# A convolution-and-attention kernel: SyncE's instructions in source order, queries prepared a slot sooner, and VectorE adding channel chunks ahead of the mean products of the first image

## The chip, the cores and the metric

The kernel runs on one core of one Trainium2 chip. A core has five engines with instruction queues of their own: TensorE (PE) multiplies matrices into PSUM, VectorE (DVE) and ScalarE (ACT) work elementwise on PSUM and SBUF, GpSimd (POOL) and SyncE (SP) here mostly issue DMAs. Each queue is worked off in order; an instruction that waits holds everything behind it. The metric is the device time of one execution in microseconds (us), as the median of several runs.

## The reference

For each of 4 images of 384 channels and 48 x 48 pixels (2304 tokens), in float32:

```python
x_flat = x.reshape(B, C, N).transpose(0, 2, 1)
local = conv_general_dilated(x, conv_w, (1, 1), 'SAME', feature_group_count=C)   # depthwise, 7 x 7
local = local * inv + (bn_beta - bn_mean * inv)                                  # batch norm
qkv = layernorm(x_flat) @ qkv_w.T + qkv_b                                        # 8 heads of 48
q = q + layernorm(local)
out = softmax(q @ k.T * 48 ** -0.5) @ v
result = x_flat + out @ proj_w.T + proj_b
```

So each query is the sum of a projection of the normalised pixel and of the normalised local convolution; the softmax runs over all 2304 tokens of the image.

## The kernel before

**Tiles and stages.** Channels lie on the 128 partitions in three chunks (`CC = 3`). An image's queries are worked in 5 tiles of 8, 10, 10, 10 and 10 pixel rows (384 or 480 tokens); `t` counts the tiles of all images, 0 to 19. Ahead of an image's tiles stands its key phase: six groups of 384 tokens (`g`, or `gk` for images 1 to 3), each making values, keys and raw queries with PE (L556, in `project`) and, for images 1 to 3, the output projection of the image before.

**Slots.** A tile has 12 slots: 4 pairs of heads times 3 parts of 6 key blocks. In a slot PE first makes six blocks of scores (`score`, L940), ScalarE takes their exponentials (L948), and PE then weighs the values with them (`weigh`, L955). The sums go to SBUF by ScalarE (L837, L847), and VectorE adds those of parts 1 and 2 (`sums_add`, L856). All of PSUM is one ring of four buffers of two banks.

**Queries.** The scores multiply at reduced width, so each query is split in a high part, a ScalarE copy (`high_queries`, L808), and a low part, a VectorE subtraction (`low_queries`, L813). SyncE then copies rows within the tile (two DMAs of L818, four of L820) so that both parts stand on the right partitions. `high_queries(t, pair + 1)` stood ahead of the scores of the second slot of a pair, `low_queries(t, pair + 1)` between its weighing and the second half of its convolution work. Pair 0 of the next tile is prepared near the end of the tile: in image 0 by the branch `early`, later by the branch `following`. At slot 0 `gather_tails` copies the fourth pair's rows (8 DMAs, L562). Keys get the same split in the key phase (L646 by ScalarE, L649 by VectorE), and `keys_out` sends the parts by SyncE (L579 to L582) and GpSimd.

**Convolution.** VectorE makes the 49 taps of three chunks, 147 instructions a tile (L306, L302), as one stream. A planner written in the kernel deals them out: every half slot and every fifth of a key group has a `room` in microseconds, every tile a due point, and the rate is the largest need over room. `FIRST_ROOM` is the room of the first point, `("start",)`, between the key phase of image 0 and slot 0. During the key phase of image 0 the taps are counted out by hand (`convolve_first(n)`). The first 10 taps of chunk 0 of tile 0 are made by PE.

**Norm of the convolution.** In image 0 (`early`, tiles 1 to 4, prepared during tiles 0 to 3) the mean over channels is a product with a matrix of 1/384, three chunks accumulated (`mean_kept`, then a ScalarE copy L467): one such mean of the convolution in slot `first` (8 in tile 0, 7 in tiles 1 to 3), one of the squares in the slot after. `root` takes the reciprocal root on ScalarE (L485 to L487), `newton` refines it on VectorE (L493, L494), `local_end` and `query_end` (L785, L794) make the queries. Later images (`following`, `coming`) sum across channels by VectorE and two DMAs of SyncE instead: `out` (L508 writes `parts`, L509 reads it back as `four`, and waits for it), then `few_in` (L518).

**The divisor.** `sums_add` sends the softmax sums to DRAM (L861); `divide` of a later point (slot 2 of the next tile, or key group 1 of the next image) reads them (`rd`, L876), takes the reciprocal on VectorE (L877), writes it (L882) and reads it back as a broadcast (`rb`, L887, L890), by which the tile's output is multiplied (L1246, L1134).

**What sets the order.** `tc.manual_schedule(engines=...)` names the engines whose instructions are kept in the order of the source. These were PE, VectorE and ScalarE; for the loads at the start also SyncE and GpSimd. Everything else on SyncE and GpSimd is put in an order by the framework's planner, which simulates the program. It may set a DMA that is ready early ahead of others that stand before it in the source.

Of the kernel before, what the change touches and what calls it, by code (L numbers as in the profile page):

```python
# [29 lines left out]
OUT_SLOT = 7  # L30
WARM = 14
PE_TAPS = 10
FIRST_ROOM = 14.0

# [11 lines left out]
def unshifted_pass(  # L48
# [16 lines left out]
    nc = tc.nc  # L65
# [7 lines left out]
    NP = NH // 2  # L73
# [20 lines left out]
    work = ctx.enter_context(tc.tile_pool(name="work", bufs=2))  # L94
    dram = ctx.enter_context(tc.tile_pool(name="dram", bufs=2, space=bass.MemoryType.DRAM))
    ps = ctx.enter_context(tc.tile_pool(name="ps", bufs=4, space=bass.MemoryType.PSUM))
    engines = {mybir.EngineType.PE, mybir.EngineType.DVE, mybir.EngineType.Activation}
    ctx.enter_context(tc.manual_schedule(engines=engines))

    def two_banks(name="r"):  # L100
        return ps.tile([P, 2, 512], F32, tag="r", name=name)
# [21 lines left out]
    def load_slab(b, g, parts=1, queue=nc.gpsimd):  # L123
# [7 lines left out]


    loads = ExitStack()
    loads.enter_context(
        tc.manual_schedule(engines={mybir.EngineType.SP, mybir.EngineType.Pool})
    )
    nc.scalar.preload_act_table_set("natural_log_exp_and_others")


# [15 lines left out]
    mean_w = const.tile([P, P], F32, tag="mean_w", name="mean_w")  # L155
# [110 lines left out]
    accs = {}  # L266
# [140 lines left out]
    def convolve(*point):  # L407
        for _ in range(share[point]):
            next(stream)
# [6 lines left out]
    class Norm:  # L416
# [41 lines left out]
        def mean_by_chunk(self, src, m=None):  # L458
            self.m = two_banks()[:, 0, : self.n] if m is None else m
            project(self.m, lambda c: mean_w, lambda c: src[:, c, :])  # L460

        def mean_kept(self, src):

            m = two_banks()[:, 0, : self.n]
            project(m, lambda c: mean_w, lambda c: src[:, c, :])
            self.m = self.buf[:, 0, :]
            nc.scalar.copy(self.m, m)  # L467

        def mean_of(self, src, at):

# [333 lines left out]
    def high_queries(t, p):  # L804
        qs = work.tile([P, 3, GM], HALF, tag="qs", name=f"qs{t}_{p}", bufs=5)
        qs = qs[:, :, : columns_of(t)]
        stacked[t, p] = qs
        nc.scalar.copy(qs[:, 0, :], query_of(t, p))  # L808
# [40 lines left out]
    def sums_add():  # L849

        if not parts_of:
            return
        t, p, i, part = parts_of.popleft()
        ao, ao3, den = outputs[t]
        dst = (ao[:, p, :] if p < CC else ao3)[0 : 64 + HA]
        nc.vector.tensor_add(dst, dst, part[0 : 64 + HA])  # L856
        if i < KB // BATCH - 1:
            return
        for j in range(2):
            r = 64 * j  # L860
            nc.sync.dma_start(out=den[2 * p + j : 2 * p + j + 1], in_=dst[r + HD : r + HA])  # L861
        if p == NP - 1:
            for c in range(CC):
                for r in (0, 64):
                    nc.sync.dma_start(
                        out=ao[r + HD : r + 64, c, :], in_=ao3[r + 16 * c : r + 16 * c + 16]
                    )
# [95 lines left out]
    def score_batch(t, s):  # L963
        p, k0 = s // (KB // BATCH), s % (KB // BATCH) * BATCH
        for kb in range(k0, k0 + BATCH):
            score(t, p, kb)
# [17 lines left out]
    def convolve_first(n):  # L984
        nonlocal n_first
        n_first += n
        for _ in range(n):
            next(stream)
# [62 lines left out]
    for g in range(1, NG):  # L1051

        last = g == NG - 1
        making = from_x(0, g)
        both(making)
        assert not last or n_first >= each - PE_TAPS
        norm = Norm(accs[0] if last else xn[0, g + 1])
        norm.mean_by_chunk(norm.src)
        if last:
            added = output_bias()  # L1060
        if g in (3, 5):
            keep_stack(0, g // 2 - 1)
        convolve_first(8)
        norm.centre()
        norm.squares()
        both(making)
        if not last:
            convolve_first(7)
            both(making)
        norm.mean_by_chunk(norm.buf)  # L1070
        norm.root()
        if last:
            convolve_first(9)
        lows_out(1)
        if last:
            both(making)
        both(making)
        convolve_first(4 if last else 10)
        if not last:
            lows_out(2)  # L1080
        if last:
            local_end(0, norm.newton())
        else:
            norm.scale(norm.newton())
        next(making)
        if last:
            query_end(0)
            high_queries(0, 0)
            low_queries(0, 0)
        next(making)  # L1090
        if not last:
            convolve_first(7)
# [5 lines left out]
    for t in range(NT):  # L1098
# [72 lines left out]
        first, second = norm_slots(t)  # L1171
        for s in range(NSLOT):
            pair, part = divmod(s, KB // BATCH)
            if part == 1 and pair < NP - 1:
                high_queries(t, pair + 1)
            if early and s == first + 3:
                high_queries(t + 1, 0)
            score_batch(t, s)
            if s == 0:
                gather_tails(*reversed(queries[t]))  # L1180
            if s == 0 and g == 0:
                keep_stack(b, 2)
            if (s or g) and (s < NSLOT - 2 or g < NA - 1):
                load_keys(b, s + 2)
            if s == 2 and g:
                rb = divide(t - 1)
            if s == 0 and coming:
                load_x(b + 1, g - begins(b + 1))
            if s == NSLOT - 4 and g == NA - 1:
                if next_image:  # L1190
                    ao = fetch(b, 0)
                    for gx in range(NG - later(b + 1), NG - 1):
                        load_x(b + 1, gx)
                else:
                    places = [("acc", 3)] * 3 + [("sq", 2)] * 2 + [("qs", 5)]
                    aos = []
                    for i in range(NG):
                        load_residual(b, i, *places[i])
                        aos.append(fetch(b, i) if i < NG - 1 else outputs[t][0])
            if coming and s == X_SLOTS[1] + 1:  # L1200
                norm_x.scale(norm_x.few_newton())
            if following and s == second + 1:
                local_end(t + 1, norm.few_newton())
                query_end(t + 1)
                high_queries(t + 1, 0)
            if coming and s == X_SLOTS[0] + 1:
                jobs.extend(norm_x.square_jobs())
            if following and s == first + 1:
                jobs.extend(norm.square_jobs())
            if coming and s == X_SLOTS[1]:  # L1210
                norm_x.few_variance()
            if following and s == second:
                norm.few_variance()
            if early and s == first + 3:
                low_queries(t + 1, 0)
            convolve("slot", t, s, 0)
            sums_add()
            if early and s == first + 1:
                norm.centre()
                jobs.extend(norm.square_jobs())  # L1220
            if early and s == first + 2:
                local_end(t + 1, norm.newton())
                query_end(t + 1)
            if coming and s == X_SLOTS[1]:
                norm_x.few_root()
            if following and s == second:
                norm.few_root()
            weigh_batch(t, s)
            if early and s == first:
                norm = Norm(accs[t + 1])  # L1230
                norm.mean_kept(norm.src)
            if early and s == first + 1:
                norm.mean_kept(norm.buf)
                norm.root()
            if part == 1 and pair < NP - 1:
                low_queries(t, pair + 1)
            convolve("slot", t, s, 1)
            if following and s == second + 1:
                low_queries(t + 1, 0)
            if coming and s == X_SLOTS[0]:  # L1240
                norm_x.few_centre()
            if following and s == first:
                norm.few_centre()
            if s == OUT_SLOT and g:
                ao = outputs[t - 1][0]
                nc.vector.tensor_mul(ao, ao, rb)  # L1246
                hold(t - 1)
            if coming and s == X_SLOTS[0] - 2:
                norm_x = Norm(xn[b + 1, g - begins(b + 1)])
                norm_x.sum()  # L1250
                norm_x.out()
            if coming and s == X_SLOTS[0] + 1:
                norm_x.sum_squares()
                norm_x.out()
            if following and s == first - 2:
                norm = Norm(accs[t + 1])
                norm.sum()
                norm.out()
            if following and s == first + 1:
                norm.sum_squares()  # L1260
                norm.out()
# [559 lines left out]
```

## Time and profile before

| | us |
|---|---|
| runs (3) | 2777.67, 2779.15, 2781.53; median 2779.15 |
| the profiled execution | 2776.61 |
| its span | 2774.7 |
| TensorE / VectorE / ScalarE busy in it | 2738.0 / 2348.4 / 1633.0 |
| mean granted TensorE clock | 0.996 |

The kernel is timed by the runs; the profile shows one execution. In it a line such as `L306 DVE ...` gathers all instructions of one source line, engine, operation and shape, with the engine's busy time and the mean duration of one. A wait is told as "who waited, <- for whom: total us, times, longest". "DVE ... <- ACT ..." is an engine that waited for another; "<- DMA" for a transfer's landing. SyncE's own instructions appear as `SPq`: they wait and issue, and do not count as busy. In this profile image 0's key phase ends at about 165 us and its tiles at 729 us. A slot of PE lasts 9.07 us in a tile of 480 tokens and 7.38 us in one of 384, and in images 1 to 3 every slot but the first of an image has this length.

### The profile page before, as it was taken

Reading aid. Unit: us, or ns where it says so; the run is one execution under the profiler, and the core shown is the slowest. Engines: PE = TensorE matmul, PEld = TensorE weight load, DVE = VectorE, ACT = ScalarE, POOL = GpSimd, SP = SyncE. Lnnn points to the kernel's source line nnn. Section 1 sums busy time; section 2 is a strip of 40 time slices with the busy share of each in tenths; the row PEclk is TensorE's granted clock in tenths of the full one; section 3 lists DMA queues with packets and bytes.
Section 4 is the critical chain, followed back from the end, with each engine's and each line's share of the span. In section 5 each row is a group of like instructions: output and inputs, shape, how many; then the busy total and the mean of one; then the engine's idle time right before and its main releaser. Section 6 shows DMA issues by size and latency. Waiting matters only on the chain.

```text
span 2774.7 us, 46317 instructions
## 1 busy us (share of the span) xinstructions
PE 2738.0 (99%) x16402; PEld 1552.4 (56%) x16402; DVE 2348.4 (85%) x4100; ACT 1633.0 (59%) x2262; POOL 695.5 (25%) x1273
## 2 busy tenths in 40 slices
PE   9989999999999999999999999999999999999999
PEld 6555555555555655555556555555555565555555
DVE  7998988989999999989888899898899889987212
ACT  4346666666424676776732567677652276676662
POOL 5641101111375111110257311101117711110110
PEclk9999999999999999999999999999999999999999
DMA  7345534445455454454545554545535545444442
GB/s 142 94 117 133 138 108 126 127 121 143 129 151 151 127 149 132 128 136 133 158 125 145 150 141 122 138 126 145 138 117 166 136 133 132 141 127 133 142 147 73
DMA packets 163297, 369.14 MB, mean 133 GB/s; under 512 B 61488, under 2 KB 112208, under 8 KB 163056
## 3 DMA queue, kind: packets, MB, share of 16 engines
q0 software_dynamic: 76992, 284.75, 35.8%
q1 hardware_dynamic: 83072, 77.72, 12.2%
q10 hardware_dynamic: 2992, 3.62, 0.4%
q8 instruction: 132, 2.16, 0.3%
q14 instruction: 109, 0.89, 0.1%
HBM read 258.14 MB, written 64.14 MB: 116 GB/s over the span
## 4 chain that ended last, share of the span: by engine, by line
PE 86%; DVE 5%; POOL 4%; DMA 3%; issue 1%; ACT 1%; SPq 0%; DVEq 0%; ACTq 0%; POOLq 0%
PE o L955 41%; PE r L940 33%; PE r L556 11%; DVE acc L306 3%; DMA wide<-k 1%; POOL wide L582 1%; POOL wide L607 1%; DMA slab<-in_x_dram 1%; POOL wide L580 1%; DMA qs<-qs 1%; DVE k L649 0%; POOL wide L579 0%; POOL wide L601 0%; DVE xn L794 0%; DMA ks<-k 0%
## 5 line engine op out<-in xcount | busy, mean ns | idle before, releaser
L306 DVE SCALAR_TENSOR_TENSOR acc<-slab,vec,acc 128x470 f32<-128x470 f32 (+9 forms) x2871 | 1687.8, 657 | 1.2
L948 ACT ACTIVATE pt<-r 128x960 f32<-128x960 f32 (+1 forms) x1440 | 1248.8, 943 | 247.0 <-PE o L955 149.6
L955 PE MATMUL o<-pt,v 128*64 128x480 f32 (+1 forms) x5760 | 1166.2, 554 | 3.9 <-ACT pt L948 3.9
L940 PE MATMUL r<-qs,ks 64*128 64x480 f32 (+1 forms) x8640 | 974.5, 375 | 18.0 <-DMA qs<-qs 12.9
L940 PEld LDWEIGHTS r<-qs,ks 64*128 64x128 f32 x8640 | 789.0, 185 | 284.8 <-issue 170.6
L955 PEld LDWEIGHTS o<-pt,v 128*64 128x64 f32 x5760 | 392.0, 137 | 663.1 <-issue 580.7
L616 POOL DMA_DIRECT2D ks<-wide x228 | 165.5, 726 | 1363.9 <-PE r L940 1326.8
L556 PE MATMUL r<-xn,w_qk 128*128 128x384 f32 x864 | 283.7, 486 | 0.0
L837 ACT COPY o<-o 113x480 f32<-113x480 f32 (+1 forms) x160 | 87.1, 544 | 299.7 <-PE o L955 299.7
L556 PEld LDWEIGHTS r<-xn,w_qk 128*128 128x128 f32 x864 | 164.2, 190 | 114.5
L856 DVE TENSOR_TENSOR ao<-ao,o 113x480 f32<-113x480 f32 (+1 forms) x120 | 76.1, 634 | 104.2 <-ACT o L837 104.1
L556 PE MATMUL r<-w_v,xn 128*128 128x384 f32 x432 | 146.7, 492 | 4.6 <-DVE xn L551 4.6
L638 ACT COPY v<-r 128x384 f32<-128x384 f32 x72 | 32.1, 480 | 197.2 <-PE r L556 197.2
L556 PEld LDWEIGHTS r<-w_v,xn 128*128 128x128 f32 x432 | 82.2, 192 | 64.4 <-issue 8.0
L582 POOL DMA_DIRECT2D wide<-k x192 | 96.6, 508 | 9.2 <-issue 7.2
L607 POOL DMA_DIRECT2D wide<-k x192 | 93.2, 491 | 1.3 <-DMA wide<-k 1.2
L847 ACT COPY ao<-o 113x480 f32<-113x480 f32 (+1 forms) x60 | 32.7, 545 | 101.5 <-PE o L955 101.5
L601 POOL DMA_DIRECT2D wide<-k x144 | 71.8, 502 | 81.5 <-ACT k L646 62.7
L556 PE MATMUL r<-af,w_o 128*128 128x384 f32 (+1 forms) x270 | 85.2, 470 | 0.0
L663 ACT ACTIVATE xn<-r,qkb 128x384 f32<-128x384 f32 x72 | 41.1, 578 | 67.4 <-PE r L556 65.9
L108 POOL DMA_DIRECT2D slab<-in_x_dram x76 | 46.2, 614 | 125.6 <-DVE acc L306 125.6
L813 DVE TENSOR_TENSOR qs<-xn,qs 128x480 fp32r<-128x480 f32 (+1 forms) x60 | 37.9, 632 | 46.6 <-ACT qs L808 46.6
(135 smaller groups left out, 1319.8 us busy)
## 6 DMA issues: line engine op xcount, KB each, us to landing
ks<-wide POOLq DMA_DIRECT2D x228, 768.0 KB, 5.2
qs<-qs SPq DMA_DIRECT2D x352, 60.0 KB
wide<-k POOLq DMA_DIRECT2D x480, 24.0 KB, 2.0
slab<-in_x_dram POOLq DMA_DIRECT2D x24, 432.0 KB, 7.1
wide<-k POOLq DMA_DIRECT2D x192, 48.0 KB, 1.8
wide<-ks POOLq DMA_DIRECT2D x12, 768.0 KB, 4.3
xr<-in_x_dram POOLq DMA_DIRECT2D x16, 576.0 KB, 5.5
rb<-rden SPq DMA_DIRECT2D x32, 270.0 KB
```

The lines of the kernel that those rows point to most:

```text
L108: queue.dma_start(out=dst[p0 : p0 + piece.shape[0]], in_=piece)
L306: nc.vector.scalar_tensor_tensor(dst, src, weight, dst, ALU.mult, ALU.add)
L556: nc.tensor.matmul(dst, lhsT=weights(c), rhs=src(c), start=c == 0, stop=c == CC - 1)
L582: queue.dma_start(out=dst[r + 32 * i : r + 32 * i + 32, 1], in_=k[r + 16 : r + HD, 1])
L601: nc.gpsimd.dma_start(out=last[16 * u : 16 * u + 16, 0], in_=k[r : r + 16, 0])
L607: nc.gpsimd.dma_start(out=last[to : to + 16, 1], in_=k[r : r + 16, 1])
L616: nc.gpsimd.dma_start(out=place_keys(b, p, i), in_=wide[b, p][:, :, at])
L837: nc.scalar.copy(part[0 : 64 + HA], sums[0 : 64 + HA, 0, :n])
L856: nc.vector.tensor_add(dst, dst, part[0 : 64 + HA])
L940: nc.tensor.matmul(r[:, j, :n], lhsT=ks[rows, w, at], rhs=qs[rows, m, :], start=i == 0, stop=i == 2,)
L948: nc.scalar.activation(pt, r[:, :, :n], AF.Exp, scale=SCALE)
L955: nc.tensor.matmul(sums[halves[j], 0, : columns_of(t)], lhsT=values[t // NA, kb // NB][:, first : first + 64], rhs=pt[:, j, :], start=i == ...
```

## The change

It has four parts.

1. SyncE joins the engines that keep the order of the source, for the whole program; GpSimd stays with the planner outside the loads.
2. The next pair's queries are prepared one slot sooner: the high part behind the scores of a pair's first slot, the low part and its DMAs at that slot's end, behind both halves of its convolution work.
3. In image 0, VectorE adds the three chunks ahead of one mean product: for the convolution in all of tiles 0 to 3 (`norm.sum()`, then `mean_of_sum`), for the squares in tiles 1 to 3. There the squares' mean moves from slot `first + 1` to `first + 2`, newton and the query's end from `first + 2` to `first + 3`, the next tile's high part behind that slot's weighing and its low part to that slot's end. In tile 0 the squares' mean and what follows stay as they were.
4. Fewer taps ahead of slot 0: three fewer in each of groups 1 to 4 (8, 7, 10, 7 become 7, 6, 9, 7), and `FIRST_ROOM` from 14 to 4.

```diff
-FIRST_ROOM = 14.0
+FIRST_ROOM = 4.0
...
-    engines = {mybir.EngineType.PE, mybir.EngineType.DVE, mybir.EngineType.Activation}
+    engines = {
+        mybir.EngineType.PE,
+        mybir.EngineType.DVE,
+        mybir.EngineType.Activation,
+        mybir.EngineType.SP,
+    }
...
-    loads.enter_context(
-        tc.manual_schedule(engines={mybir.EngineType.SP, mybir.EngineType.Pool})
-    )
+    loads.enter_context(tc.manual_schedule(engines={mybir.EngineType.Pool}))
...
+        def keep(self, m):
+            self.m = self.buf[:, 0, :]
+            nc.scalar.copy(self.m, m)
+
         def mean_kept(self, src):
 
             m = two_banks()[:, 0, : self.n]
             project(m, lambda c: mean_w, lambda c: src[:, c, :])
-            self.m = self.buf[:, 0, :]
-            nc.scalar.copy(self.m, m)
+            self.keep(m)
+
+        def mean_of_sum(self):
+
+            m = two_banks()[:, 0, : self.n]
+            nc.tensor.matmul(m, lhsT=mean_w, rhs=self.buf[:, 0, :], start=True, stop=True)
+            self.keep(m)
...
-        convolve_first(8)
+        convolve_first(8 if last else 7)
...
         if not last:
-            convolve_first(7)
+            convolve_first(6)
...
-        convolve_first(4 if last else 10)
+        convolve_first(4 if last else 9)
...
-            if part == 1 and pair < NP - 1:
-                high_queries(t, pair + 1)
-            if early and s == first + 3:
+            if t == 0 and s == first + 3:
                 high_queries(t + 1, 0)
             score_batch(t, s)
+            if part == 0 and pair < NP - 1:
+                high_queries(t, pair + 1)
...
-            if early and s == first + 3:
+            if t == 0 and s == first + 3:
                 low_queries(t + 1, 0)
             convolve("slot", t, s, 0)
             sums_add()
+            if early and s == first:
+                norm = Norm(accs[t + 1])
+                norm.sum()
             if early and s == first + 1:
                 norm.centre()
                 jobs.extend(norm.square_jobs())
-            if early and s == first + 2:
+            if early and s == first + (2 if t == 0 else 3):
                 local_end(t + 1, norm.newton())
                 query_end(t + 1)
...
             weigh_batch(t, s)
             if early and s == first:
-                norm = Norm(accs[t + 1])
-                norm.mean_kept(norm.src)
-            if early and s == first + 1:
+                norm.mean_of_sum()
+            if t == 0 and s == first + 1:
                 norm.mean_kept(norm.buf)
                 norm.root()
-            if part == 1 and pair < NP - 1:
+            if t and early and s == first + 2:
+                norm.mean_of_sum()
+                norm.root()
+            if t and early and s == first + 3:
+                high_queries(t + 1, 0)
+            convolve("slot", t, s, 1)
+            if part == 0 and pair < NP - 1:
                 low_queries(t, pair + 1)
-            convolve("slot", t, s, 1)
+            if t and early and s == first + 1:
+                norm.sum_squares()
+            if t and early and s == first + 3:
+                low_queries(t + 1, 0)
```

## The prediction

> **What bounds the kernel now.** I read, in order, the busy times, the waits, the granted clock, and the timelines of the engines around each wait.
>
> The busy line of the page:
>
> ```profile
> PE 2738.0 (99%) x16402; PEld 1552.4 (56%) x16402; DVE 2348.4 (85%) x4100; ACT 1633.0 (59%) x2262; POOL 695.5 (25%) x1273
> ```
>
> TensorE (PE) works 2738.0 of 2774.7 us. A microsecond is won by giving it fewer products, or by removing one of its few waits; the other engines matter only where PE waits for them. The list of PE's waits shows how few there are (total, times, longest):
>
> ```profile
> PE r L940 <- DMA qs<-qs: 12.9, 8, 3.6
> PE r L556 <- DVE xn L551: 4.6, 2, 2.9
> PE o L955 <- ACT pt L948: 3.9, 3, 1.8
> PE r L940 <- ACT pt L948: 3.2, 4, 1.1
> ```
>
> The longest, 3.6 us, is at slot 3 of tile 0. VectorE comes first to the low query part of pair 1 (L813), at 189.21, and SyncE's copies follow:
>
> ```profile
> 189.21 0.55 DVE L813 TENSOR_TENSOR qs<-xn,qs 128x384 fp32r<-128x384 f32 x1
> ...
> 191.78 0.59 SPq L820 DMA_DIRECT2D qs<-qs  x1
> ...
> 195.53 6.34 PE L940 MATMUL r<-qs,ks 64*128 64x384 f32 x36 [3.64 <-DMA qs<-qs]
> ```
>
> These 36 scores take 6.3 us. The windows tell why (PE clock is the 1.00 or 0.50 after POOL's count):
>
> ```profile
> 195.00:198.00 3.00, 2.47 (x15) 2.50 (x17) 3.00 (x6) 0.81 (x1) 0.00 (x0) 0.50 0.01 2
> 198.00:202.00 4.00, 4.00 (x27) 3.56 (x25) 4.00 (x8) 2.43 (x3) 0.00 (x0) 0.53 0.01 2
> ```
>
> So the slot lasts 14.01 us from weighing end to weighing end, against 7.38 for its neighbours: the late query costs 6.6 us, not 3.6.
>
> A mean product in a slot, on PE's timeline in tile 1:
>
> ```profile
> 341.95 5.05 PE L955 MATMUL o<-pt,v 128*64 128x480 f32 x24
> 346.93 2.68 PE L556 MATMUL r<-acc,mean_w 128*128 128x480 f32 x6
> 349.55 4.17 PE L940 MATMUL r<-qs,ks 64*128 64x480 f32 x36
> ```
>
> Three products are six records, 0.403 us from start to start. Nothing covers them: the slot is 11.69 us instead of 9.07.
>
> **What the skill says.** "TensorE: Matmul & The Clock Gate", section "What's actually happening": a window of about 3.4 us of idling drops PE to half clock, and about as much work restores it. The trace agrees: 0.50 to 0.53 after 3.64 us, 0.56 after 2.92 us (at 140), 1.00 after 2.20 us (at 274). "DMA: Bandwidth & Descriptors", section "Anatomy of one DMA": a wait is made by the issuing sequencer ahead of dispatch, and some 2 us of a DMA are fixed. The first makes SyncE's order matter: what waits there holds all behind it. The second agrees at best: small copies land 2.0 us after issue in quiet moments; by SyncE's semaphores its query copies have a median near 3.3 us and an upper quartile of 5.1.
>
> **The change, part by part.** PE's order outside the means is unchanged.
>
> *Means.* Tiles 0 to 3 replace a three-chunk mean of the convolution by one product (4 places), tiles 1 to 3 also that of the squares (3): 7 x 2 products = 28 records x 0.403 = **-11.3 us** on PE. VectorE gains 14 additions of 0.65 (row L448, 128x480): 9.2 us. In tiles 1 to 3 it idled 9 to 15 us around these slots (waiting for L467 and L487), which hides them if it arrives in time.
>
> *Fewer taps early.* Groups 1 to 4 lose 3 taps each. In groups 1 and 2 VectorE waits for PE at each centring (56.1, 77.4), so group 1's saving is lost; the other nine, at 0.61 less what the same waits eat, leave 4.9. Both waits for L551 (1.68 and 2.92 at 115.8 and 140.3) disappear, since 4.9 is more than their 4.6. What is then late is tile 0's first query: its subtraction ends 4.9 sooner, but in source order all six copies follow it, where two now go before it: two more issues of 0.63 = 1.3. Slot 0 opens 4.9 - 1.3 = **-3.6 us**.
>
> *Start and the sooner query.* By the planner's own formula the taps ahead of slot 0 go from 24 to 7 (the trace shows 40 taps between 164.8 and 189.2: 24 and the 16 of slot 0 and half of slot 1, so the formula is what runs). Pair 1's subtraction now follows 7 + 12 = 19 taps x 0.61, about 172; its copies land by 180, ahead of slot 3. **-6.6 us.** Elsewhere no query of pairs 1 to 3 made PE wait, so "one slot sooner" is worth nothing there; ScalarE's copy moves within a slot in which it is busy 5.9 of 9.07 us.
>
> *What those taps cost later.* Shares in tiles 0 to 3 go from 123, 149, 150, 143 to 133, 158, 155, 146. I added VectorE's queue in source order (0.61 a tap, 0.57 a sum, 0.65 a subtraction) against PE's slots. Before slot 7 of tile 1 it loses 9 taps + 1.3 = 6.8 us of a lead of 7.3, so the chunk sum comes when PE wants it: 0 to 1.2, I take 0.6. In tile 0 the squares come 0.7 late. For tile t+1's first query (tiles 1 to 3: root after slot 9, newton after slot 10's first taps, then 7 or 8 taps, L813) the subtraction ends some 33 us after slot 7, PE wants it at 39.5: four issues to the last L818 and 3.3 to land make 39 for tiles 2 and 3 (no wait). For tile 4, with 6 more taps and the next image's norm ahead, they make 42.4: 2.9. Tile 1 already waits 2.2; one more tap adds 0.7. The reciprocal of slot 2 may wait for its copy behind slot 0's 22 issues of SyncE (22 x 0.64 = 14 us of 18): 0.4. Sum **+5.3**; with landings of 5.1 and half clock after the two longer waits, +11.6.
>
> *SyncE in source order, images 1 to 3.* In key group 1, `divide` issues rd<-den behind `out`, whose second DMA waits for the first. SyncE before:
>
> ```profile
> 758.79 0.55 SPq L508 DMA_DIRECT2D parts<-part  x1
> 759.44 0.43 SPq L882 DMA_DIRECT2D rden<-rd  x1
> 764.13 0.56 SPq L509 DMA_DIRECT2D four<-parts  x1
> ```
>
> rd<-den had been issued at 735.7, so the reciprocal ran at 759.02. In source order it goes out behind 764.13, at about 764.8, and lands 2.8 later (as at the end of the kernel, 2740.0 to 2742.9): the reciprocal is D = 8.6 us late. Behind it on VectorE stand 8 taps, three key parts (L649, which free PSUM) and the scaling L551. PE's next use allows 3.25 us in image 1 (772.57 to 775.82) and VectorE's own idle 1.25 takes more; images 2 and 3 allow 6.5 and 6.8. PE loses 4.1 + 2.1 + 1.3 (the part lands sooner in image 3) = **+7.5**. A gain is excluded; the upper end is D = 13, +21.
>
> *Image starts.* The planner put 7 tail copies and 6 key copies ahead of the first query; source order puts 7 key copies, then six query copies. Counting issues, the last L818 goes 1.2 sooner in image 1 (0.9 of it useful), 0.7 and 0.9 later in 2 and 3: **+0.7**. GpSimd stays the planner's: the slab at 221.8 held the keys behind it until 222.96, and they landed at 230.3, 4.7 ahead of need. With convolution 1 ending two slots later that can be 0 or 7 us; I take 0, as the planner moves the slab too.
>
> Sum: -11.3 - 3.6 - 6.6 + 5.3 + 7.5 + 0.7 = **-8.0 us** on the profiled 2776.61, 2768.6. The median of the runs is 2.5 above the profiled time, so **2771**.
>
> **The rivals.**
> *Given back (0.30).* Landings at the upper quartile and half clock after waits near 3 us: image 0 keeps 21.5 - 11.6 = 9.9, later images take 8.7: -1, 2778. For it: L818 issued at 268.75 took 5.5 to land beside a key load. Against: most small copies land faster.
> *Slower (0.20).* One mechanism: VectorE's reciprocal stuck behind SyncE's L509 in each key group 1. PE loses about 3D - 17.8; from waits near 3 us on, half clock adds 1.8 an image (as at 140). At D = 12 that is 18.2 + 5.4, 16 more than I charged: +8, 2787. Slower than 0.2% from D = 11.2. For it: part and rden both took some 5 us to land there, beside loads of xr and af. Against: these loads have landed (763.8) when rd goes out.
> *The change does not act.* If the planner's SyncE order already was the source's, nothing of the 7.5 is lost: -16, 2763. The issue of rd at 735.7 speaks against it; it stays in the low end.
>
> **How the numbers follow.** My forecast has 0.50, its own range 2760 to 2773; given back 0.30; slower 0.20. Runs tell 0.2% (5.6 us) from no change. The range 2760 to 2787 leaves one in ten below (no loss at SyncE) and one in ten above. Faster 0.50, same 0.30, slower 0.20.
>
> **What would show it.** Right: slot 3 of tile 0 lasts 7.4; slots 7 of tiles 1 to 3 last 10.1, slots 8 9.1; no wait for L551 in image 0; "DVE rd L877 <- DMA rd<-den" grows from 6.6 to about 30; PE waits 1 to 4 us in key group 1 of images 1 to 3; tile 4 opens with a query wait. Wrong: rd issued ahead of L509; VectorE leading by microseconds at slot 7 of tile 1; PE waiting for keys (ks) behind a slab; PE at half clock in places I have not named.

## The result and the profile after

The changed kernel takes 2771.45 us in the median of 7 runs (2768.67 to 2772.5) against 2781.53 for the kernel before in the same comparison. The ratio is 0.9961 with a 95% interval of 0.9949 to 0.9973: faster by 0.39%, clear of the 0.2% that can be told from no change. The forecast was 2771.0, faster. The profiled execution fell from 2776.61 to 2768.89 us.

Line numbers after the change are some 3 to 12 higher: L551 became L563, L649 L661, L813 L825, L818/L820 L830/L832, L876/L877 L888/L889, L940 L952, L948 L960, L955 L967, L508/L509 L520/L521.

The busy line of the page after:

```profile
PE 2728.2 (99%) x16374; PEld 1547.9 (56%) x16374; DVE 2354.3 (85%) x4114; ACT 1638.4 (59%) x2262; POOL 695.0 (25%) x1273
```

PE made 28 records fewer and was busy 9.8 us less (2738.0 before). VectorE made 14 instructions more, for 5.9 us. The list of PE's waits after (total, times, longest; qs are the parts of the queries, pt the exponentials, xn the normalised pixels, k the key parts):

```profile
PE r L952 <- DMA qs<-qs: 13.3, 11, 2.5
PE o L967 <- ACT pt L960: 4.6, 2, 2.7
...
PE r L568 <- DVE xn L563: 2.4, 2, 1.9
...
PE r L568 <- DVE k L661: 1.5, 2, 0.8
```

The total for queries is unchanged (12.9 before), but these are other waits: 11 short ones, and none of 3.6 us. The waits for L563 halved in total and moved: they stood in image 0's key phase, and the larger one now stands in image 1's key group 1, where one for L661 is new. Slot 3 of tile 0, on PE's timeline:

```profile
189.83 3.43 PE L952 MATMUL r<-qs,ks 64*128 64x384 f32 x36
193.19 4.09 PE L967 MATMUL o<-pt,v 128*64 128x384 f32 x24
```

No wait, and 36 scores in 3.4 us where they took 6.3. The mean product of slot 7 of tile 1 on the same view is two records long, not six:

```profile
338.38 1.07 PE L478 MATMUL r<-sq,mean_w 128*128 128x480 f32 x2
339.38 4.17 PE L952 MATMUL r<-qs,ks 64*128 64x480 f32 x36
```

Key group 1 of image 1, SyncE's timeline:

```profile
744.45 0.57 SPq L520 DMA_DIRECT2D parts<-part  x1
749.35 0.55 SPq L521 DMA_DIRECT2D four<-parts  x1
749.95 0.47 SPq L888 DMA_DIRECT2D rd<-den  x1
752.80 0.33 SPq L894 DMA_DIRECT2D rden<-rd  x1
```

`parts` lands 4.9 us after its issue, L521 waits for it, and rd<-den goes out only behind L521. Before, rd<-den had gone out ahead of the group, and the reciprocal ran without a wait (SyncE and VectorE of the kernel before):

```profile
735.68 0.47 SPq L876 DMA_DIRECT2D rd<-den  x1
...
759.02 0.34 DVE L877 RECIPROCAL rd<-rd 128x30 f32<-128x30 f32 x1
```

After, VectorE's timeline shows what the place of rd<-den costs it, and PE's what arrives there:

```profile
752.43 0.34 DVE L889 RECIPROCAL rd<-rd 128x30 f32<-128x30 f32 x1 [7.66 <-DMA rd<-den]
```
```profile
758.61 4.14 PE L568 MATMUL r<-af,w_o 128*128 128x384 f32 x12 [0.85 <-DVE k L661]
764.69 1.56 PE L568 MATMUL r<-w_v,xn 128*128 128x384 f32 x4 [1.95 <-DVE xn L563]
```

The time by stage, read from the start of the last weighing product of a slot in both profiled executions (us):

| last weighing product of | before | after | difference so far |
|---|---|---|---|
| slot 0 of tile 0 | 176.7 | 174.7 | -2.0 |
| slot 3 of tile 0 | 205.4 | 196.8 | -8.6 |
| slot 11 of tile 0 | 271.2 | 260.9 | -10.3 |
| slot 0 of tile 1 | 282.9 | 274.4 | -8.5 |
| slot 11 of tile 1 | 389.2 | 377.4 | -11.8 |
| slot 11 of tile 4 (image 0 ends) | 728.8 | 714.4 | -14.4 |
| slot 0 of tile 5 (image 1) | 880.8 | 870.4 | -10.4 |
| slot 0 of tile 10 (image 2) | 1548.5 | 1539.2 | -9.3 |
| slot 0 of tile 15 (image 3) | 2217.1 | 2209.4 | -7.7 |
| slot 11 of tile 19 | 2733.8 | 2726.1 | -7.7 |

Image 0 wins 14.4 us. The key phases of images 1 to 3 give back 4.0, 1.1 and 1.7.

### The profile page after: what moved, and what is told of

Same layout as the page of the kernel before. It is cut to its first block, busy times and chain, and to the rows that moved or that the text cites. A ratio compares the mean times of both kernels' runs of the same rounds, so it can differ in the third digit from the quotient of the medians.

```text
span 2767.1 us, 46151 instructions
## 1 busy us (share of the span) xinstructions
PE 2728.2 (99%) x16374; PEld 1547.9 (56%) x16374; DVE 2354.3 (85%) x4114; ACT 1638.4 (59%) x2262; POOL 695.0 (25%) x1273
## 3 DMA queue, kind: packets, MB, share of 16 engines
q1 hardware_dynamic: 83072, 77.72, 12.5%
q8 instruction: 132, 2.16, 0.3%
## 4 chain that ended last, share of the span: by engine, by line
PE 83%; DVE 6%; DMA 5%; POOL 3%; issue 1%; SPq 1%; ACT 1%; DVEq 0%; ACTq 0%; POOLq 0%
PE o L967 40%; PE r L952 33%; PE r L568 9%; DVE acc L309 3%; DMA wide<-k 1%; POOL wide L594 1%; DMA qs<-qs 1%; DMA slab<-in_x_dram 1%; POOL wide L619 1%; DMA parts<-part 1%; DVE k L661 0%; POOL wide L592 0%; DVE xn L806 0%; DVE acc L797 0%; POOL wide L613 0%
## 5 line engine op out<-in xcount | busy, mean ns | idle before, releaser
L960 ACT ACTIVATE pt<-r 128x960 f32<-128x960 f32 (+1 forms) x1440 | 1249.2, 943 | 272.7 <-PE o L967 151.4
L967 PE MATMUL o<-pt,v 128*64 128x480 f32 (+1 forms) x5760 | 1166.2, 554 | 4.6 <-ACT pt L960 4.6
L952 PE MATMUL r<-qs,ks 64*128 64x480 f32 (+1 forms) x8640 | 976.7, 375 | 19.2 <-DMA qs<-qs 13.3
L952 PEld LDWEIGHTS r<-qs,ks 64*128 64x128 f32 x8640 | 790.6, 185 | 286.6 <-issue 178.1
L967 PEld LDWEIGHTS o<-pt,v 128*64 128x64 f32 x5760 | 392.1, 137 | 663.6 <-issue 570.3
L825 DVE TENSOR_TENSOR qs<-xn,qs 128x480 fp32r<-128x480 f32 (+1 forms) x60 | 38.2, 637 | 65.3 <-ACT qs L820 65.3
L868 DVE TENSOR_TENSOR aot<-aot,o 113x480 f32<-113x480 f32 (+1 forms) x40 | 25.6, 640 | 56.8 <-ACT o L849 56.6
```

What stands on the lines that cost most here:

```text
L952: nc.tensor.matmul(r[:, j, :n], lhsT=ks[rows, w, at], rhs=qs[rows, m, :], start=i == 0, stop=i == 2,)
L960: nc.scalar.activation(pt, r[:, :, :n], AF.Exp, scale=SCALE)
L967: nc.tensor.matmul(sums[halves[j], 0, : columns_of(t)], lhsT=values[t // NA, kb // NB][:, first : first + 64], rhs=pt[:, j, :], start=i == ...
```

## The experiments

All ratios are to the kernel before, each run beside it; two of them differ with some confidence from about 0.0018 (5 us) on. A ratio difference of 0.001 is 2.8 us. Where a comparison has to be finer, the stage table is read, whose slots repeat within 0.1 us where no wait differs.

**SyncE given back to the planner** (`u1_planner`): the changed kernel without its first part.

```diff
-        mybir.EngineType.SP,
...
-    loads.enter_context(tc.manual_schedule(engines={mybir.EngineType.Pool}))
+    loads.enter_context(
+        tc.manual_schedule(engines={mybir.EngineType.SP, mybir.EngineType.Pool})
+    )
```

> The changed kernel with its first part undone: SyncE's instructions are ordered by the planner again, the other three parts stay. Theory (source order holds rd<-den behind the waiting second DMA of `out` in key group 1 of images 1 to 3): rd goes out ahead of L521 there, the waits of TensorE for key parts and L563 in key group 1 disappear, images 1 to 3 together give back the 6.8 us that they take in the changed kernel, image 0 stays as it is: about 2765 against 2771.5. Rival (the source order also brings image 0's query copies out sooner, so that the planner's order costs there what it wins later): 2769 to 2775, with longer waits for qs in image 0.

Measured: 2760.83 us, ratio 0.9916 (0.9902 to 0.9929): 0.0045 or 12.5 us less than the changed kernel, 10.6 by the medians. SyncE's timeline in key group 1 of image 1:

```profile
740.68 0.55 SPq L521 DMA_DIRECT2D parts<-part  x1
741.35 0.41 SPq L895 DMA_DIRECT2D rden<-rd  x1
746.03 0.56 SPq L522 DMA_DIRECT2D four<-parts  x1
```

(lines one higher than in the changed kernel). rden<-rd is out before the waiting DMA L522 is: rd had long landed. The waits of PE in key group 1 of images 1 and 3 are gone, image 1's key phase lasts 151.5 instead of 156.0. The profiled execution, the slowest of the five, shows less than the runs (4.7 us at the end): its image 2 opened with a wait of 3.9 us for pt. By the runs the source order costs more than the 6.8 us that the stage table gives it; image 0 too is 3.7 us shorter here, 1.4 of it by the end of slot 0 and the rest at the first slots of tiles 1 to 4.

**The means undone** (`u3_means`): three-chunk products and the old places in tiles 0 to 3.

```diff
-            if early and s == first:
-                norm = Norm(accs[t + 1])
-                norm.sum()
...
-            if early and s == first + (2 if t == 0 else 3):
+            if early and s == first + 2:
...
-                norm.mean_of_sum()
-            if t == 0 and s == first + 1:
+                norm = Norm(accs[t + 1])
+                norm.mean_kept(norm.src)
+            if early and s == first + 1:
```

> The changed kernel with its third part undone: three-chunk mean products in image 0, no additions on VectorE ahead of them, the squares' mean in slot first + 1 and the query's end in first + 2 for all of tiles 0 to 3. Theory (28 product records of 0.403 us are the gain, the additions are nearly hidden): 11.3 us more on TensorE, less what the waits at the first slots of tiles 1 to 4 shrink (at most 6): 2777 to 2783 against 2771.5, the 28 records back. Rival (VectorE's 14 additions and the later query cost what the products save): within 3 us of 2771.5, the first slots of tiles 1 to 4 without waits.

Measured: 2779.37 us, ratio 0.9989 (0.9982 to 0.9996): 7.8 us slower than the changed kernel. Slots with one product less are 1.60 us shorter each in the changed kernel (slot 9 of tile 0: 8.37 against 9.98; slots 8 and 10 of tiles 1 to 3: 10.09 and 11.29 against 11.69 and 12.89), seven times, 11.2 us. Image 0 as a whole lasts only 6.4 us longer here, because tiles 2 to 4 open without a wait. So the means are worth 11.2 on PE, and about 5 of it is paid back at the next tile's first query.

**The taps undone** (`u4_taps`): 24 taps ahead of slot 0 again.

```diff
-FIRST_ROOM = 4.0
+FIRST_ROOM = 14.0
...
-        convolve_first(8 if last else 7)
+        convolve_first(8)
...
-            convolve_first(6)
+            convolve_first(7)
...
-        convolve_first(4 if last else 9)
+        convolve_first(4 if last else 10)
```

> The changed kernel with its fourth part undone: 8, 7, 10, 7 taps in the key groups of image 0 and FIRST_ROOM 14, so 24 taps ahead of slot 0. Theory (fewer taps are what removed the late query of slot 3): the low part of pair 1 comes behind 36 taps where it came behind 40, the wait at slot 3 of tile 0 is 1 to 1.5 us and without half clock, the waits for L563 of 1.7 and 2.9 in image 0's key phase are back, slot 0 opens some 2 us later, and tiles 1 to 4 open sooner: 2771 to 2776. Rival (the sooner query alone removed it): slot 3 lasts 7.4, and the time stays within 2 us of 2771.5.

Measured: 2779.31 us, ratio 0.9990 (0.9983 to 0.9996), 8.1 us slower, more than either theory gave. Slot 0 ends 2.9 later, slot 3 lasts 11.11 us, 3.7 more. PE's timeline there:

```profile
192.72 1.12 PE L952 MATMUL r<-qs,ks 64*128 64x384 f32 x5
195.29 4.59 PE L952 MATMUL r<-qs,ks 64*128 64x384 f32 x31 [1.46 <-DMA qs<-qs]
```

The wait is the 1.5 us expected, but the clock fell to 0.50 all the same, which makes up the other 2.2. So of the 6.6 us that the change wins at slot 3, fewer taps bring 3.7 here.

**The sooner query undone** (`u2_queries`).

```diff
...
-            if part == 0 and pair < NP - 1:
-                high_queries(t, pair + 1)
...
+            if part == 1 and pair < NP - 1:
+                low_queries(t, pair + 1)
             convolve("slot", t, s, 1)
-            if part == 0 and pair < NP - 1:
-                low_queries(t, pair + 1)
```

> The changed kernel with its second part undone: pairs 1 to 3 are prepared in the second slot of the pair before, as in the kernel before; fewer taps stay. Theory (with 7 taps ahead of slot 0 the low part of pair 1 comes behind some 24 taps, at about 177, and is in time without being sooner): slot 3 of tile 0 lasts 7.4 us and the time stays within 3 us of 2771.5. Rival (the sooner query is needed with the source order, since SyncE's other copies stand ahead): waits for qs at slots 3, 6 and 9 appear, 5 us or more slower.

Measured: 2783.41 us, ratio 1.0009 (1.0001 to 1.0017): 13.3 us slower than the changed kernel. The theory fell. Slot 3 of tile 0 indeed lasts 7.4. But tile 1 (0.8 us) and tiles 6 and 7, in image 1, now wait for queries at slot 6 (1.1 us at 1014.5; 2.0 and 3.1 at 1126 to 1130, a slot of 16.97 us). VectorE's list of waits has 20 for rd, where the changed kernel has 16 (59.3 us in all):

```profile
DVE rd L889 <- DMA rd<-den: 101.4, 20, 8.3
```

The profiled execution was the slowest of the 13 (2790.02 us), so its waits may be longer than those of the median run.

**The source order alone** (`b1_source`): the kernel before with the first part.

```diff
-    engines = {mybir.EngineType.PE, mybir.EngineType.DVE, mybir.EngineType.Activation}
+    engines = {
+        mybir.EngineType.PE,
+        mybir.EngineType.DVE,
+        mybir.EngineType.Activation,
+        mybir.EngineType.SP,
+    }
...
-        tc.manual_schedule(engines={mybir.EngineType.SP, mybir.EngineType.Pool})
+        tc.manual_schedule(engines={mybir.EngineType.Pool})
```

> The kernel before with the first part alone: SyncE in the order of the source, nothing else. Theory (the source order costs the same with or without the other parts, by rd<-den in key group 1 and by the copies at the starts of images and tiles): 8 to 13 us slower than before, ratio 1.003 to 1.0045; VectorE's waits for rd grow from 6.6 us to over 30, image 1's key phase grows most. Rival (it costs only beside the other parts, which fill VectorE's lead): within 3 us of before.

Measured: 2798.2 us, ratio 1.0055 (1.0043 to 1.0068): 15 us slower, over the theory's range. Besides key group 1, slots inside tiles lose here. Tile 7, on SyncE, VectorE and PE:

```profile
1106.41 0.35 SPq L879 DMA_DIRECT2D rd<-den  x1
1113.70 0.35 SPq L885 DMA_DIRECT2D rden<-rd  x1
```
```profile
1113.33 0.34 DVE L880 RECIPROCAL rd<-rd 128x30 f32<-128x30 f32 x1 [6.74 <-DMA rd<-den]
```
```profile
1142.19 0.79 PE L943 MATMUL r<-qs,ks 64*128 64x480 f32 x4 [1.70 <-DMA qs<-qs]
1144.93 1.57 PE L943 MATMUL r<-qs,ks 64*128 64x480 f32 x6 [1.94 <-DMA qs<-qs]
```

In the source, rd<-den of slot 2 stands behind the six copies of the late query of slot 1. It lands 6.9 us after its issue, VectorE stands 6.7 us for it, is busy without a break in the slots that follow, and comes to the low part of pair 2, which belongs in slot 4, at 1134.07, in slot 5; the copies land past the start of slot 6. Under the planner, in the kernel before, rd<-den goes out ahead of those copies, and VectorE doesn't wait in this tile:

```profile
1082.92 0.54 SPq L876 DMA_DIRECT2D rd<-den  x1
```

**An early rd<-den** (`i1_rd`): the changed kernel with the load in key group 0.

```diff
+                if gk == 0:
+                    divisor_in(t - 1)
                 lows_out(1)
...
-        nc.sync.dma_start(out=rd, in_=outputs[t][2].rearrange("h (k f) -> (h k) f", f=few))
         nc.vector.reciprocal(rd, rd)
```

(`divisor_in` makes the tile `rd` and issues this DMA.)

> The changed kernel with one DMA moved: in images 1 to 3 rd<-den is issued in key group 0, ahead of its first low key part, instead of in `divide` in key group 1 behind the second DMA of `out`. Theory (this DMA is the whole cost of the source order in key group 1): the reciprocal of key group 1 waits less than 1 us, TensorE's waits for L661 and L563 in group 1 disappear, 3 to 5 us won: about 2767. Rival (the waiting second DMA of `out` costs by what else stands behind it, the key copies): the reciprocal comes in time and the total stays within 1.5 us of 2771.5.

Measured: 2766.01 us, ratio 0.9934 (0.9921 to 0.9948), 7.5 us less than the changed kernel by the ratios and 5.4 by the medians. No wait for L661 or L563 is left in key group 1; image 0 ends at 714.5, as before this edit (714.4). Image 1's key phase lasts 153.9 instead of 156.0, image 2's and 3's 0.1 and 0.8 less. At the start of image 3 PE waits longer for pt instead (3.5 us where it was 1.9): part of the gain goes there.

**Early rd<-den with the late query** (`u2_rd`): `u2_queries`, `i1_rd`, and the load in the tiles at the end of slot 0.

```diff
             convolve("slot", t, s, 1)
+            if s == 0 and g:
+                divisor_in(t - 1)
```

> The changed kernel without the sooner query (second part undone, as in u2_queries), and rd<-den issued early everywhere: in key group 0 of images 1 to 3, and at the end of slot 0 of the tiles that divide, instead of in slot 2. Theory (in source order rd<-den is issued late in slot 2, VectorE stands 5 to 8 us in each of these slots for it, and what it loses makes the late queries of image 1's tiles miss their slots): VectorE's wait for rd falls from 101 us to under 20, the waits for qs inside the tiles of image 1 go away, and most of the 12 us that u2_queries is slower than the changed kernel comes back, with the key group's 3 to 5 us on top: 2766 to 2770. Rival (the six copies of a query are late behind SyncE's other copies, and not because VectorE is): the waits for qs stay, 2778 or more.

Measured: 2764.78 us, ratio 0.9953 (0.9940 to 0.9967): 15.6 us less than `u2_queries`. VectorE's list of waits:

```profile
DVE rd L899 <- DMA rd<-den: 3.7, 2, 2.0
```

3.7 us instead of 101.4, and no wait for queries inside a tile of images 1 to 3 is left. This separates the two causes: the late queries of `u2_queries` were late because VectorE was, and VectorE was late because of where rd<-den stood in SyncE's order. In the changed kernel the key group's load alone gave 7.5 us (`i1_rd`), so not all of the 15.6 stands inside tiles. With the load early, the late query of `u2_rd` and the sooner one of `i1_rd` end 5.3 us apart by the ratios and 1.2 the other way by the medians, so what the sooner query is worth there is not settled.

**The sooner query alone** (`b2_queries`): the kernel before with the second part, under the planner's order.

```diff
...
+            if part == 0 and pair < NP - 1:
+                high_queries(t, pair + 1)
...
-            if part == 1 and pair < NP - 1:
-                low_queries(t, pair + 1)
             convolve("slot", t, s, 1)
+            if part == 0 and pair < NP - 1:
+                low_queries(t, pair + 1)
```

> The kernel before with the second part alone: the queries of pairs 1 to 3 one slot sooner, SyncE left to the planner, taps as before. Theory (under the planner's order only slot 3 of tile 0 has a late query, and there the low part comes 4 taps sooner): slot 3 falls from 14.0 to about 11.1 as in u4_taps, all other slots as before: 2 to 4 us faster, ratio 0.9985 to 0.9993. Rival (a query that is sooner also wins elsewhere): over 6 us faster.

Measured: 2777.21 us, ratio 0.9990 (0.9982 to 0.9999), 2.8 us. The time is as expected, the place is not: slot 3 lasts 7.38, all of its 6.6 us won, and slot 6 of tile 0 waits 1.6 us in its turn and falls to half clock (10.87 us), so that 3.3 are left by slot 8.

**First queries sooner** (`i3_all`): `i1_rd` and three moves.

```diff
                 query_end(t + 1)
+                high_queries(t + 1, 0)
...
-            if t and early and s == first + 3:
-                high_queries(t + 1, 0)
+            if early and s == first + (2 if t == 0 else 3):
+                low_queries(t + 1, 0)
             convolve("slot", t, s, 1)
...
-        convolve_first(4 if last else 9)
         if not last:
+            convolve_first(9)
             lows_out(2)
...
             low_queries(0, 0)
+            convolve_first(4)
...
                 both(making)
+                if gk == 5:
+                    low_queries(t, 0)
+                    lows_out(3)
                 convolve("kv", t, gk, 2)
```

(the old places of these calls fall away.)

> SyncE in source order, the early rd<-den of the run before, and three moves of the first queries: in image 0 the next tile's high part stands ahead of the weighing of slot 10 and its low part ahead of the second half of that slot's taps; ahead of slot 0 of tile 0 four taps move behind the query; in key group 5 of images 1 to 3 the low query part and all three low key parts move ahead of the taps of both middle stretches. Theory (those copies are late because VectorE and ScalarE come to them late): waits for qs at the first slots of tiles 1 to 4 go away (6 us with their half clock), slot 0 of tile 0 opens 2.5 to 4 sooner, the image starts lose 1 to 2 us each of their waits: 2750 to 2756 against 2766 of the early rd alone. Rival (the landing of the copies or the buffers of pt, held by the keys' transfers, is what lasts): 2760 to 2765.

Measured: 2749.84 us, ratio 0.9888 (0.9873 to 0.9902). The waits at the first slots of tiles 1 to 4 are gone, and those at the image starts too but for 0.7 us and less, pt's among them. Two came in their place:

```profile
PE r L478 <- DVE sq L452: 4.2, 2, 3.2
PE o L977 <- ACT pt L970: 3.3, 1, 3.3
```

The chunk sum of tile 1 is 3.2 us late (the slot lasts 16.12 instead of 10.09 us, half clock with it), and slot 0, now open sooner, waits for pt buffers that the key parts still hold.

**The same moves under the planner** (`p_all`): as above, with the first part undone and rd<-den in `divide`.

> The same three moves of the first queries with the first part undone: SyncE ordered by the planner, rd<-den left in `divide`. Theory (what the moves win does not depend on the order on SyncE): 8 to 11 us less than the 2760.8 of the planner's order alone, 2750 to 2753, with no wait for L563 or L661 in key group 1. Rival (the planner's order had already taken what the moves win): 2757 to 2761.

Measured: 2747.74 us, ratio 0.9878 (0.9864 to 0.9892): 10.6 us less than `u1_planner` by the ratios. `i3_all` stands 12.8 under `i1_rd`. As far as 5 us can tell, what the moves win does not hang on SyncE's order.

**Both new waits taken away** (`i4_all`, and `p_all2` under the planner).

```diff
-FIRST_ROOM = 4.0
+FIRST_ROOM = 9.0
...
             local_end(0, norm.newton())
+            lows_out(2)
...
             convolve("slot", t, s, 1)
+            if s == 0 and g:
+                divisor_in(t - 1)
```

(the last edit in `i4_all` alone.)

> As i3_all, with three more moves: rd<-den at the end of slot 0 also in the tiles that divide, FIRST_ROOM 9 in place of 4, and the last two low key parts of image 0 between the scaling and the query's end. Theory: the wait for the chunk sum in slot 7 of tile 1 (3.2 us and half clock in i3_all) and TensorE's wait for pt in slot 0 (3.3 us) shrink to under 1 us each; the rd loads in the tiles bring nothing, since VectorE's stalls there are hidden: 4 to 7 us less than i3_all, 2743 to 2746. Rival (taps ahead of slot 0 delay the query of slot 3 again, and the low key parts delay the first query by as much as they win): 2748 to 2752.

> As p_all (SyncE by the planner), with FIRST_ROOM 9 and the last two low key parts of image 0 between the scaling and the query's end. Theory: the wait for pt in slot 0 (3.2 us) and for the chunk sum in tile 1 (1.3 us) shrink, the first query comes 1.1 us later: 2 to 5 us less than p_all, 2743 to 2746. Rival (the first query's delay eats it): 2747 to 2750.

Measured: `i4_all` 2742.7 us, ratio 0.9866 (0.9851 to 0.9881), the lowest ratio of all and 1.34% under the kernel before. Its list of PE's waits:

```profile
PE r L962 <- ACT pt L970: 3.2, 4, 1.1
PE r L478 <- DVE sq L452: 2.2, 2, 1.1
...
PE r L962 <- DMA qs<-qs: 2.1, 2, 1.6
```

The wait for pt in slot 0 is gone, tile 1's late sum too; sums in tiles 0 and 2 are 1.1 late. The tiles of image 1 take 516.7 us in `i3_all` and in `i4_all`, while VectorE's wait for rd fell from 34.5 to 7.6 us: with the sooner query, those stalls were hidden. `p_all2` took 2745.08 us, 0.9878 (0.9863 to 0.9893): by the ratio no less than `p_all`, 2.7 less by the medians. A chunk sum of tile 0 came 2.6 us late there, with half clock, which ate much of what slot 0 won.

## Why the prediction was right, and where it was wrong

The terms of the sum against the profiled executions (us):

| term | predicted | measured |
|---|---|---|
| means | -11.3 | -11.2 (7 x 1.60) |
| slot 0 of tile 0 opens | -3.6 | -2.0 |
| slot 3 of tile 0 | -6.6 | -6.6 |
| tile 0's late squares, tile 1's late sum, rd at slot 2 | +1.7 | 0 |
| first queries of tiles 1 to 4 | +0.7, 0, 0, +2.9 | +1.8, +1.7, +1.0, +1.2 |
| key phases of images 1 to 3, both terms | +3.2, +2.8, +2.2 | +4.0, +1.1, +1.7 |
| sum | -8.0 | -7.7 (at the last slot; the rows add to -7.3) |

**The total.** That it came out so closely is in part luck. The forecast of 2771 was counted from 2779.15, the median of the three runs then known; the seven have 2781.53, and the kernel moved by 10.1 us by the medians and 10.8 by the ratio, not by 8.0. By the runs, `u1_planner`, the change without its first part, stands 23.3 us under the kernel before, where the prediction counted 16.2 for those parts, and the first part costs 12.5, where it charged 8.2: two misses of opposite sign. The profiled executions show 12.4 for the former; which term holds the rest stays open.

**Means.** Right to 0.1, by counting records on PE's timeline. The extra VectorE work was hidden in its own slots, as said, and paid for at the next query.

**Slot 0.** The key phase ended 4.9 sooner on PE, as worked out. The subtraction ended only 3.1 sooner: this execution stood 0.95 later from its first loads on (first centring of group 1 at 57.06 against 56.11), and the nine taps left 4.0 where 4.9 were counted. The copy that opened the slot landed 3.5 us after issue, where it took 2.6 before. The order of the copies, charged 1.3, cost 0.3, since the copy that mattered was the fourth of six.

**Slot 3.** The size is right, and the two edits overlap. Fewer taps take all of the 6.6 without the sooner query (`u2_queries`); the sooner query takes all of it under the planner (`b2_queries`) and 2.9 of it in source order (`u4_taps`). They don't add.

**First queries.** They cost 5.7 against 3.6, and the row above it nothing against 1.7, so that the sum of the two is right (5.7 against 5.3) by luck: the places are not. I took one landing of 3.3 us for all of them. The copies that ended these waits landed 5.0, 5.6, 4.9 and 5.4 us after issue. Tile 1 also fell to half clock after a wait of 2.35, which I had placed on the safe side. Tile 4 was better than counted.

**Key group 1.** The mechanism is as predicted and `i1_rd` shows it: moving that one DMA removes the waits. The reciprocal was 7.7 us late, not 8.6, and PE lost 2.8 in image 1, nothing in image 2, 0.7 in image 3; the rest of the key phases' loss stands at the image starts. By the runs the whole first part costs more than the 8.2 charged, so the profiled pair flatters this term.

**The step that failed: "one slot sooner is worth nothing there" and rd at slot 2 for 0.4.** I priced the late rd<-den in slot 2 by SyncE's issues alone, and took from the trace of before that no query of the later pairs is late. That trace has the planner's order. In source order VectorE waits for rd in 16 of 20 places after the change (59.3 us in all, 22 of them in key groups 1) and in all 20 with the late query (over 100), where I wrote 30, and only the sooner query keeps the waits inside tiles from PE. `u2_queries` prices this cover at 13.3 us, `b2_queries` the same edit at 2.8 under the planner. The predicted time was not hurt, because both edits come together; taken singly, I would have missed them by some 7 and 13 us.

**The rivals.** "Does not act" is excluded by rd<-den at 749.95. "Slower" needed a reciprocal 11.2 us late; it was 7.7. "Given back" was right that landings near 5 us and half clock would come; they came in four first slots and cost 2 us over the plan.

**The signs named.** Slot 3 of 7.4: yes. Slots of 10.1: yes, counted by weighing ends as slot 8, since the product stands behind slot 7's weighing. No wait for L551 in image 0: one of 0.45 us is left (136.9). Waits in key group 1 in all of images 1 to 3: in two of them. Tile 4 opening with a wait: 0.75 us, and so do tiles 1 to 3. One sign of being wrong came: half clock in places not named, at the first slot of tile 1 (0.50 from 265.01 to 268.42) and at the start of image 2 (0.50 from 1531.35 to 1534.77).

## What to carry to other kernels

Before an engine's queue is put in source order, look for every instruction that it can run early and that another engine needs at once: one load left behind other DMAs cost VectorE up to 8 us a time, and with that load placed by hand, and the first queries sooner in both, the source order and the planner's can no longer be told apart (2742.7 against 2745.1 us). An edit that moves work sooner is worth what the other edits make late: price it in their company, and not by the waits of the old trace. And a wait that is removed shows the next one at once: each step from `i1_rd` to `i4_all` had to be read from a new list of waits.

## What was not expected of the hardware

How long PE waits does not decide whether it falls to half clock; how much of the wait lies in one window does. In each of the 14 profiles the granted clock changes only at times that lie a whole number of 3.413 us apart, so that one change gives the places of all windows of a run. Here are PE's windows, cut at these places (us, busy, granted clock, DMA share, GB/s), around two waits of the same 2.16 us at the first slot of tile 1. In `i1_rd` (a wait from 261.30 to 263.46):

```profile
258.90:262.31 3.41, 2.40 (x15) 1.00 0.91 291
262.31:265.72 3.41, 2.26 (x20) 1.00 0.34 72
```

and in `u1_planner` (from 260.44 to 262.60):

```profile
260.56:263.97 3.41, 1.38 (x12) 1.00 0.29 62
263.97:267.38 3.41, 3.41 (x21) 0.50 0.00 0
```

The edge of a window cuts the first wait in 1.0 and 1.2 us, and PE keeps its clock. Of the second, 2.04 us lie in one window; the whole next window has half clock, and the slot is 1.6 us longer. Counted over the 14 profiles, from 100 us to the end, in whole windows that began at full clock: in 53 PE stood for 1.95 us or more in all, and each of these was followed by a window at 0.50. No window in which it stood for less than 1.48 us was. Between the two, 17 of 46 were, and what decides there stays open.

So waits of 2.20 (kernel before), 2.43 and 3.08 us (`u2_rd`) left the clock at 1.00 and cost 0.5 to 0.7 us over the wait itself, while waits of 1.46 and 1.54 (`u4_taps`) and 2.35 (changed kernel) did not and cost 2.1 to 2.3 over. The 3.08 was cut in 1.67 and 1.41; the 1.46 lay whole in one window. The prediction's use of a threshold between 2.20 and 2.92 was wrong. The Trainium skill ("TensorE: Matmul & The Clock Gate", section "What's actually happening") says that the window of about 3.4 us over which activity is judged is free-running, so that it depends on where work falls in it; the traces agree. That a window in which PE was busy for 1.90 of 3.41 us (`u4_taps`, from 192.91) is enough does not fit its other statement, that a whole idle window is needed; the measurement decides. The windows stand elsewhere in each run (the first change of the clock comes at 7.23 us in the kernel before, at 5.59 in the changed one), so a forecast can't place them: a wait of 1.5 to 3 us on PE costs itself and either some 0.5 or some 2 us more, an estimate from the slots above.
